# Norms pinned in program order, gate matmuls spread out, and list numbers multiplied in on ScalarE: one edit of a linear-attention and mixture-of-experts kernel

## The chip, the cores and the metric

The kernel runs on one core of a Trainium2 chip, with its engines TensorE (PE), VectorE (DVE), ScalarE (ACT), GpSimd (POOL) and SyncE (SP, which issues most DMAs). The metric is the device time of one execution in microseconds (us), the median of several runs. Every engine takes its instructions in the order of the built program, so an instruction that waits holds up those behind it on its engine.

## The reference

The input `x` is 8 x 512 x 512 (batch, token, channel), float32. All of it is computed in float32:

```python
xn = layernorm(x)
# attention, 16 heads of 32, in chunks of 128 tokens
q, k, v = rotate(silu(xn @ Wq)), rotate(silu(xn @ Wk)), xn @ Wv
o = lightning_attention(q, k, v)          # per chunk: (q k^T * decay) v + (q * decay) state
o = group_rmsnorm(o * sigmoid(xn @ Wg1 @ Wg2)) * norm_weight
s = o @ Wo
# mixture: 16 experts, 4 per token, and one shared expert
probs = softmax(xn @ gate_w.T); top 4, weights normalised to 1
mixed = sum over experts of weight * (silu(xn @ Wg) * (xn @ Wu)) @ Wd
g = silu(mixed + shared(xn) * sigmoid(xn @ shared_gate_w))
return x + s * g
```

There are 4096 tokens, so 16384 pairs of token and expert.

## The kernel before

The program is one stream of helper calls that a scheduling layer turns into one queue per engine. The order of PE's matmuls is written out by hand: `on_pe` ties each to the matmul traced before it. On the other engines the layer may reorder, by its own reckoning of when an instruction becomes ready, unless a helper says `behind(engine)`, which ties an instruction to the last one traced on that engine. Accumulators in PSUM come from `bank(tag, ...)`: tag `a` has four banks, `d` two, `m` and `k` one each. A matmul into a bank waits until whoever read its last content is done.

**Stage 1, to about 220 us.** For each batch `b`, `first()` yields pieces: `route_1` (router logits, L305, copied to `lT` at L309), `share_1` (the shared expert's gate and up matmuls, L358, with silu on ACT and the product `h` on DVE, L364), `norm(b + 2)`, `turn(b + 1)` (transposes, L289, copied by ACT at L291), `route_2` (top 4, softmax and one-hot masks: L317 to L348) and `share_2` (L374, four tiles of tokens whose results `sh` are taken out by ACT for even tiles, L380, and by DVE for odd ones, L378, then written to DRAM). `norm` computes statistics on DVE (L250, L252), the inverse root on POOL (L254, L256), and centres on DVE (L242). `along()` hands out nine pieces for every five calls, between the pieces of the first batch's attention: `value(0, t)` for four tiles (L574), then the gates `gate_1`, `gate_2`, `gate_3` of batch 0 (L587, L596, L608, results copied or put through a sigmoid by ACT: L591, L598, L611), then `enter` and `sequence(0)`: keys and queries (L619, silu at L624, rotation on DVE at L626 to L630), `by_token` (L646, L649), `scores` (L664, L675, and on DVE L678, L680, L685, L691), `output` (L703, L709, and on DVE L713). In `norm`, `stand` ties the instructions of batches 0 and 1 with `behind`, those of later batches not.

`sort()` then gives each pair its place in a list ordered by expert, in blocks of 128.

**Stage 2, about 249 to 330 us.** `table(room)` turns places into `slot`, the token that stands at each place. There are 128 lists (4 ranks x 32 tiles of 128 tokens), in 8 groups of 16. For each group `make` builds on DVE, in f16, one-hot rows of the place within a block (`place`, L510: 1024 wide for 8 lists), multiplies them by the token number (L512), and builds one-hot rows of the block (`block`, L515: 1144 wide); the lists lie next to each other, so one list's row is every fourth element. PE multiplies `place` by `block` per list (L534, into `pn`, bank `a`) and DVE adds the groups up (L540, L542). Two groups have room at a time. `filling` is the generator of all this, and `between[0]` advances it once after each matmul of `value` and `rotated`, inside `sequence(1)`. `sequence(1)` begins with `scores(1, 0)`, goes on with `key(1, 2)`, and then calls `gate_3(1)`, which needs four banks `a` that the scores have just used.

```python
        make(0)
        for _ in range(KC + 1):
            yield
        for i in range(0, TOPK * NT, GROUP):
            if i + GROUP < TOPK * NT:
                make(i + GROUP)
```

**Afterwards** the expert weights (`wexp`, loaded while stage 2 runs) are applied to 136 blocks of gathered rows (L1026 to L1097), and the attention of batches 2 to 7 runs on PE while gathered expert results are added up and joined with it (L1164 to L1202).

Of the kernel before, what the change touches and what calls it, by code (L numbers as in the profile page):

```python
# [11 lines left out]
F16 = mybir.dt.float16  # L12
# [4 lines left out]
ALU = mybir.AluOpType  # L17
# [34 lines left out]
def shape_constants():  # L52

    f = np.float32
    c = {}
    lam = -(f(2.0) ** (f(-8.0) * (np.arange(H, dtype=f) + f(1.0)) / f(H))).astype(f)
    i = np.arange(C, dtype=f)
    diff = i[None, :] - i[:, None]
    dec = np.exp(lam[None, :, None] * np.maximum(diff, f(0.0))[:, None, :])
    c["dmask"] = np.where(diff[:, None, :] >= 0, dec, f(0.0))  # L60
    dq = np.exp(lam[:, None] * (i[None, :] + f(1.0)))
    c["dq"] = np.repeat(dq.reshape(G, HG, 1, C), HD, axis=2).reshape(G, P, C).transpose(1, 0, 2)
    c["dk"] = np.exp(lam[None, :] * (f(C) - f(1.0) - i[:, None]))
    lc = np.exp(lam * f(C))
    c["lamc"] = np.repeat(lc.reshape(G, HG, 1), HD, axis=2).reshape(G, P).T
    half = HD // 2
    theta = (f(BASE) ** (f(-2.0) * np.arange(half, dtype=f) / f(HD))).astype(f)
    ang = (np.arange(N, dtype=f)[None, :] * theta[:, None]).astype(f)
    c["cos"] = np.tile(np.cos(ang), (2 * HG, 1))
    c["sin"] = np.tile(np.concatenate([-np.sin(ang), np.sin(ang)], axis=0), (HG, 1))  # L70
    c["ident"] = np.eye(P)


    sel = np.zeros((P, H - HG + Q))
    exp = np.zeros((H, G, P))
    for g in range(G):
        for j in range(HG):
            sel[j * HD : (j + 1) * HD, H - HG + j] = 1.0 / HD
            exp[g * HG + j, g, j * HD : (j + 1) * HD] = 1.0
    c["sel"] = sel  # L80

    c["four"] = np.tile(np.eye(Q), (P // Q, P // Q))
    c["fold"] = np.tile(np.eye(Q)[:, :EA], (P // Q, 1))

    c["tri"] = np.triu(np.ones((P, P)), 1)
    c["iota_e"] = np.tile(np.arange(E), (P, 1))
    c["reset"] = np.tile((np.arange(NT) > 0)[None], (P, E)).reshape(P, E * NT)
    out = {k: np.ascontiguousarray(v.reshape(P, -1), dtype=f) for k, v in c.items()}
    out["exp"] = exp.reshape(H, D).astype(f)
    out["iota_b"] = (np.arange(P, dtype=f)[:, None] // Q * NBQ + np.arange(NBQ, dtype=f)).astype(f)  # L90

    out["whole"] = np.tile(np.arange(NB), (P, 1)).astype(np.float16)
    out["token"] = (
        np.arange(NT)[None, :] * P + np.arange(P)[:, None] - B * N // 2).astype(np.float16)
    return out


# [1 line left out]
def tile_block(ctx: ExitStack, tc: tile.TileContext, a: dict, out: bass.AP):  # L99
# [8 lines left out]
    def bank(tag, name):  # L108
        return pp.tile([P, 512], F32, tag=tag, name=name, bufs={"a": 4, "k": 1, "m": 1, "d": 2}[tag])
# [9 lines left out]
    def load(pool, name, shape, dt=F32):  # L119
        t = pool.tile(shape, dt, tag=name, name=name, bufs=1)  # L120
        flat = t if len(shape) == 2 else t.rearrange(
            "p a b -> p (a b)" if len(shape) == 3 else "p a b c -> p (a b c)")
        nc.sync.dma_start(flat, a[name])
        return t
# [36 lines left out]
    iota_e = load(p1, "iota_e", [P, E])  # L161
    tri = load(p1, "tri", [P, P])
    reset = load(p1, "reset", [P, E * NT])
    token = load(const, "token", [P, NT], F16)
    whole = load(const, "whole", [P, NB], F16)
    iota_b = load(p1, "iota_b", [P, NBQ])
    ones = p1.tile([P, P], F32, tag="ones", name="ones")
# [48 lines left out]
    def behind(engine):  # L216

        last = next(
            (i for i in reversed(nc.cur_bb.bb.instructions) if i.engine == engine), None)
        return tc.issue_after(last) if last else nullcontext()  # L220
# [9 lines left out]
    def norm(b):  # L230
        xs = xs_of[b]
        mv = p1.tile([P, NC, 2], F32, tag="mv", name=f"mv_{b}", bufs=2)
        rstd = p1.tile([P, NC], F32, tag="rstd", name=f"rstd_{b}", bufs=2)
        tiles = [slice(t, t + 1) for t in range(NC)] if b == 0 else [slice(0, NC)]

        def stand(engine):
            return behind(engine) if b < 2 else nullcontext()

        def center(ts):
            for t in range(ts.start, ts.stop):  # L240
                with stand(DVE):
                    nc.vector.tensor_scalar(  # L242
                        xs[:, t, :], xs[:, t, :], mv[:, t, 0:1], rstd[:, t : t + 1],
                        ALU.subtract, ALU.mult)

        for i, ts in enumerate(tiles):
            for t in range(ts.start, ts.stop):
                st = p1.tile([P, 6], F32, tag="st", name=f"st_{b}_{t}", bufs=4)
                with stand(DVE):
                    nc.vector.bn_stats(st, xs[:, t, :])  # L250
                with stand(DVE):
                    nc.vector.bn_aggr(mv[:, t, :], st)  # L252
            with stand(POOL):
                nc.gpsimd.tensor_scalar(rstd[:, ts], mv[:, ts, 1], LN_EPS, None, ALU.add)  # L254
            with stand(POOL):
                nc.gpsimd.tensor_tensor(  # L256
                    rstd[:, ts], rstd[:, ts],
                    root.to_broadcast([P, ts.stop - ts.start]), ALU.pow)
            if i:
                center(tiles[i - 1])  # L260
        center(tiles[-1])
        nc.sync.dma_start(
            xn_d[b * N : (b + 1) * N, :D].rearrange("(t p) d -> p t d", p=P),
            xs[:, :, : D // 2].bitcast(U16))
# [102 lines left out]
    def share_2(b):  # L367
        h, sg = h1_of.pop(b), sg_of.pop(b)
        xT1_of.pop(b)
        for t in range(NC):  # L370
            sh = p1.tile([P, D], F32, tag="sh1", name=f"sh1_{b}_{t}", bufs=6)
            py = bank("dmaa"[t], f"pys_{b}_{t}")
            with on_pe():
                nc.tensor.matmul(  # L374
                    py, lhsT=h[:, t * P : (t + 1) * P], rhs=sw[:, KC * 2 * F :],
                    start=True, stop=True)
            if t % 2:
                nc.vector.tensor_scalar(sh, py, sg[:, t : t + 1], None, ALU.mult)  # L378
            else:
                nc.scalar.activation(sh, py, AF.Copy, scale=sg[:, t : t + 1])  # L380
            nc.sync.dma_start(sh_d[b][t * P : (t + 1) * P, :], sh)
# [91 lines left out]
    def table(room):  # L473
# [26 lines left out]
        def make(i):  # L500
            place, block = homes[i // GROUP % 2]
            for u in range(0, quads, 2):
                us = slice(u, u + 2)
                lists = slice(i + u * QUAD, i + (u + 2) * QUAD)
                first = lists.start % NT

                def counts(n):
                    return count[:, :n].unsqueeze(1).to_broadcast([P, 2, n, QUAD])

                nc.vector.tensor_tensor(  # L510
                    place[:, us], counts(P), rows(sp[:, 0, lists], P), ALU.is_equal)
                nc.vector.tensor_tensor(  # L512
                    place[:, us], place[:, us], rows(token[:, first : first + 2 * QUAD], P),
                    ALU.mult)
                nc.vector.tensor_tensor(  # L515
                    block[:, us], counts(NB), rows(sp[:, 1, lists], NB), ALU.is_equal)

        make(0)
        for _ in range(KC + 1):
            yield  # L520
        for i in range(0, TOPK * NT, GROUP):
            if i + GROUP < TOPK * NT:
                make(i + GROUP)
            else:
                for e in range(E - LATE, E - LATE // 2):
                    nc.sync.dma_start(wexp[:, e, :], a["experts"][:, e, :])
            if i < TOPK * NT // 2:
                yield
            place, block = homes[i // GROUP % 2]
            pn = bank("a", f"pn_{i}")  # L530
            for some in ((0, 5), (5, 10), (10, GROUP)):
                with on_pe():
                    for j in range(*some):
                        nc.tensor.matmul(  # L534
                            pn[:, :NB], lhsT=place[:, j // QUAD, :, j % QUAD],
                            rhs=block[:, j // QUAD, :, j % QUAD], start=(j == 0),
                            stop=(j == GROUP - 1))
                if some[1] == GROUP:
                    if i:
                        nc.vector.tensor_tensor(acc, acc, pn[:, :NB], ALU.add)  # L540
                    else:
                        nc.vector.tensor_copy(acc, pn[:, :NB])  # L542
                yield
# [427 lines left out]

    for t in range(NC):
        value(0, t)
        along()
    gate_1(0)
    gate_2(0)
    gate_3(0)
    along()
    enter(0, along)
    sequence(0, along, spill, also=lambda: next(sorting, None))  # L980
# [323 lines left out]
```

## Time and profile before

| what | value |
|---|---|
| runs | 1227.79, 1227.75, 1227.76 us, median 1227.76 |
| the profiled execution | 1224.5 us, of which the span from first to last instruction 1222.7 |
| granted TensorE clock, mean over the span | 0.991 |
| PE busy, 0 to 400 us | 373.3 us |
| DVE busy, 240 to 300 us | 53.6 of 60 us |
| ACT busy, 240 to 300 us | 10.7 of 60 us |

Busy time is the time in which an engine executes; a share of the span averages over stages with different limits. A row of instructions gives line, engine, operation, output and inputs, shape and number, then busy time and mean duration in ns, then the idle time of the engine just before them and what ended it. A row of waits gives who waited, for whom, the total in us, how often, and the longest. In the view of single stretches the columns are the stretch, its length, then busy time and number of instructions for PE, PE's weight loads, DVE, ACT and POOL, then the granted clock of TensorE (1.00 is full), the busy share of the DMA engines and GB/s. In the timeline a row begins with its start and its duration in us, and ends with the idle time before it in brackets.

### The profile page before, as it was taken

The numbers are of one execution on the slowest core, as the hardware profiler recorded it, in microseconds if no ns is written. First come the engines' busy times: TensorE is split into PE (matmuls) and PEld (weight loads), VectorE is DVE, ScalarE is ACT, GpSimd is POOL, SyncE is SP. The second block draws the span as 40 slices with busy tenths as digits, with TensorE's granted clock in tenths as the row PEclk, the third lists the DMA queues.
The fourth block names the chain that finished last, engine by engine and source line by source line (L and its number), as shares of the span: only waits on it lengthen the run. The fifth ranks groups of instructions, "written<-read, shape, count | busy, mean of one in ns | idle before, by whom it ended". The sixth has DMA issues, their size and how long they took to land. (4 is left out here: it accounts for less than half of the span.)

```text
span 1222.7 us, 21290 instructions
## 1 busy us (share of the span) xinstructions
PE 1171.0 (96%) x7708; PEld 688.6 (56%) x7708; DVE 758.6 (62%) x1632; ACT 407.2 (33%) x767; POOL 438.3 (36%) x424
## 2 busy tenths in 40 slices
PE   6998999989999999999999999999999999999997
PEld 3434554446567777777777775545544444445453
DVE  6487554889324344444444435959879689698784
ACT  3343333320274344444444432041141221411420
POOL 3122002100213333333333332832876837848211
PEclk9998999989999999999999999999999999999999
DMA  9884231182459989889998996822746626535012
GB/s 320 292 282 159 100 138 70 27 326 96 156 139 224 223 227 227 223 229 230 228 229 226 229 222 223 295 62 70 261 119 191 197 79 228 162 111 149 25 36 69
DMA packets 163352, 216.97 MB, mean 177 GB/s; under 512 B 89776, under 2 KB 98736, under 8 KB 161328
## 3 DMA queue, kind: packets, MB, share of 16 engines
q1 hardware_dynamic: 141840, 143.68, 38.9%
q0 software_dynamic: 21120, 70.34, 21.0%
q8 instruction: 64, 1.05, 0.4%
q10 hardware_dynamic: 288, 1.57, 0.4%
q14 instruction: 40, 0.33, 0.1%
HBM read 125.35 MB, written 72.35 MB: 162 GB/s over the span
## 5 line engine op out<-in xcount | busy, mean ns | idle before, releaser
L1067 PE MATMUL pgu<-wexp,xt 128*128 x1088 | 257.7, 380 | 2.3 <-ACT xt L1048 2.0
L1067 PEld LDWEIGHTS pgu<-wexp,xt 128*128 128x128 f32 x1088 | 206.0, 190 | 89.5 <-issue 43.2
L1026 POOL DMA_INDIRECT xg<-xn_d,slot x79 | 75.1, 951 | 249.8 <-DVE y L1097 163.5
L1072 DVE TENSOR_TENSOR slb<-slb,pgu 128x128 f32<-128x128 f32 x136 | 39.1, 288 | 191.0 <-ACT slb L1071 124.3
L1164 POOL DMA_INDIRECT yg<-y_d,posi x128 | 139.5, 1090 | 47.1 <-SPq L1131 19.5
L1050 ACT COPY xt<-pl 128x512 uint16<-128x512 uint16 x136 | 104.3, 767 | 126.9 <-DMA pl<-xg 70.3
L1088 PE MATMUL py<-wexp,hT 128*128 x272 | 139.3, 594 | 0.1
L574 PE MATMUL pv<-wv,xT 128*128 128x512 f32 x256 | 122.1, 613 | 4.4 <-DVE sh L378 3.0
L619 PE MATMUL pk<-xT,wk 128*128 128x512 f32 x256 | 118.3, 604 | 1.7 <-DVEq L1131 1.7
L619 PE MATMUL pq<-xT,wq 128*128 128x512 f32 x256 | 117.6, 600 | 0.0
L1196 POOL TENSOR_TENSOR xo<-xo,m 128x512 f32<-128x512 f32 x30 | 43.4, 1448 | 164.9 <-DVE m L1192 155.9
L752 PE MATMUL pw<-wo,on 128*128 128x512 f32 x224 | 100.5, 595 | 0.8 <-DVE m L1192 0.6
L1026 POOL DMA_INDIRECT more<-xn_d,slot x57 | 54.0, 947 | 109.7 <-DVE y L1097 106.8
L574 PEld LDWEIGHTS pv<-wv,xT 128*128 128x128 f32 x256 | 46.7, 195 | 59.9 <-issue 53.2
L691 DVE TENSOR_TENSOR sc<-ps,dmask 128x512 f32<-128x512 f32 x128 | 79.4, 680 | 1.0 <-PE ps L675 1.0
L619 PEld LDWEIGHTS pq<-xT,wq 128*128 128x128 f32 x256 | 47.8, 193 | 52.8 <-issue 51.7
L1097 DVE TENSOR_SCALAR y<-py,xg 128x512 f32<-128x512 f32 x79 | 59.3, 750 | 28.4 <-PE py L1088 28.0
L619 PEld LDWEIGHTS pk<-xT,wk 128*128 128x128 f32 x256 | 46.1, 190 | 52.0 <-issue 49.6
L752 PEld LDWEIGHTS pw<-wo,on 128*128 128x128 f32 x224 | 41.4, 190 | 50.5 <-issue 45.2
L1071 ACT ACTIVATE slb<-pgu 128x128 f32<-128x128 f32 x136 | 37.8, 278 | 90.9 <-PE pgu L1067 87.8
L578 ACT COPY v<-pv 128x512 f32<-128x512 f32 x32 | 18.9, 590 | 122.6 <-PE pv L574 121.8
L624 ACT ACTIVATE sk<-pk 128x512 f32<-128x512 f32 x32 | 19.1, 596 | 117.0 <-PE pk L619 100.1
(168 smaller groups left out, 1787.5 us busy)
## 6 DMA issues: line engine op xcount, KB each, us to landing
y_d<-y SPq DMA_DIRECT2D x136, 256.0 KB
wexp<-in_experts SPq DMA_DIRECT2D x14, 768.0 KB
sh_d<-sh SPq DMA_DIRECT2D x32, 256.0 KB
m<-sh_d SPq DMA_DIRECT2D x32, 256.0 KB
xo<-in_x SPq DMA_DIRECT2D x32, 256.0 KB
out<-xo SPq DMA_DIRECT2D x32, 256.0 KB
x<-in_x SPq DMA_DIRECT2D x7, 1024.0 KB
xT_d<-xT SPq DMA_DIRECT2D x7, 1024.0 KB
```

Source lines behind the costliest of these rows:

```text
L574: nc.tensor.matmul(pv, lhsT=xT_of[b][:, k, t * P : (t + 1) * P], rhs=wv[:, k, :], start=(k == 0), stop=(k == KC - 1))
L619: nc.tensor.matmul(ps, lhsT=w[:, k, g * P : (g + 1) * P], rhs=xT_of[b][:, k, :], start=(k == 0), stop=(k == KC - 1))
L691: nc.vector.tensor_tensor(s, pss[j].rearrange("p (c t) -> p c t", t=C), dmask[:, g * HG + j].unsqueeze(1).to_broadcast([P, NC, C]), ALU.mult)
L752: nc.tensor.matmul(pw, lhsT=on_of[b][:, g, t * P : (t + 1) * P], rhs=wo[:, g, :], start=(g == 0), stop=(g == G - 1))
L1026: nc.gpsimd.indirect_dma_start(out=row(i), out_offset=None, in_=xn_d, in_offset=bass.IndirectOffsetOnAxis(ap=slot[:, i : i + 1], axis=0))
L1050: nc.scalar.copy(xt[:, KP:, :].bitcast(U16).rearrange("p k (t h) -> p h k t", h=2), turned(i).rearrange("p (h k) t -> p h k t", h=2))
L1067: nc.tensor.matmul(pg[:, : 2 * F], lhsT=xt[:, k, :], rhs=wflat[:, bass.ds(off + k * 2 * F, 2 * F)], start=(k == 0), stop=(k == KC - 1))
L1072: nc.vector.tensor_tensor(sl, sl, pg[:, F : 2 * F], ALU.mult)
L1088: nc.tensor.matmul(py, lhsT=hT_of.pop(i), rhs=wflat[:, bass.ds(off_of.pop(i) + KC * 2 * F, D)], start=True, stop=True)
L1097: gone.append(nc.vector.tensor_scalar(y, py, row(i).bitcast(F32)[:, bass.ds(at, 1)], None, ALU.mult).ins)
L1164: nc.gpsimd.indirect_dma_start(out=yg, out_offset=None, in_=y_d, in_offset=bass.IndirectOffsetOnAxis(ap=posi[:, r, g : g + 1], axis=0))
L1196: nc.gpsimd.tensor_tensor(xo, xo, m, ALU.add)
```

## The change

Five edits. `norm` ties its instructions for every batch, with `behind` in place of `stand`. `share_2` takes its banks in the order `dama` in place of `dmaa`, so the tile in bank `m` is an even one. `gate_1(0)`, `gate_2(0)` and `gate_3(0)` are called after `value(0, 1)`, `value(0, 2)` and `value(0, 3)`, each ahead of `along()`, in place of all three after the last. The multiplication by the token number leaves `make`; `number` does it on ACT, one activation of 128 x 128 per list, with the token's number (now float32) as the scale: for the first group four lists at a time, one call per step, and for later ones along with the matmuls of the group before. And `filling` yields once ahead of `make(0)`, so its first step builds no rows; the steps that follow are one fewer.

```diff
     out["token"] = (
-        ... .astype(np.float16)
+        ... .astype(np.float32)
@@ norm
-        def stand(engine):
-            return behind(engine) if b < 2 else nullcontext()
-
         def center(ts):
             for t in range(ts.start, ts.stop):
-                with stand(DVE):
+                with behind(DVE):
...
-            with stand(POOL):
+            with behind(POOL):
@@ share_2
-            py = bank("dmaa"[t], f"pys_{b}_{t}")
+            py = bank("dama"[t], f"pys_{b}_{t}")
@@ table: make
-                nc.vector.tensor_tensor(
-                    place[:, us], place[:, us], rows(token[:, first : first + 2 * QUAD], P),
-                    ALU.mult)
@@ table
+        def number(i, some):
+            place = homes[i // GROUP % 2][0]
+            for j in range(*some):
+                row = place[:, j // QUAD, :, j % QUAD]
+                t = (i + j) % NT
+                nc.scalar.activation(row, row, AF.Copy, scale=token[:, t : t + 1])
+
+        yield
         make(0)
-        for _ in range(KC + 1):
+        for j in range(0, GROUP, QUAD):
+            number(0, (j, j + QUAD))
             yield
         for i in range(0, TOPK * NT, GROUP):
-            if i + GROUP < TOPK * NT:
+            more = i + GROUP < TOPK * NT
+            if more:
                 make(i + GROUP)
...
+                if more:
+                    number(i + GROUP, some)
                 if some[1] == GROUP:
@@ the calls of stage 1
     for t in range(NC):
         value(0, t)
+        if t:
+            (gate_1, gate_2, gate_3)[t - 1](0)
         along()
-    gate_1(0)
-    gate_2(0)
-    gate_3(0)
     along()
```

More of the change, by code (lines that the diff above doesn't have):

```diff
@@ L93, in shape_constants @@
     out["token"] = (
-        np.arange(NT)[None, :] * P + np.arange(P)[:, None] - B * N // 2).astype(np.float16)
+        np.arange(NT)[None, :] * P + np.arange(P)[:, None] - B * N // 2).astype(np.float32)
     return out
@@ L163, in tile_block @@
     reset = load(p1, "reset", [P, E * NT])
-    token = load(const, "token", [P, NT], F16)
+    token = load(const, "token", [P, NT])
     whole = load(const, "whole", [P, NB], F16)
@@ L248, in norm @@
                 st = p1.tile([P, 6], F32, tag="st", name=f"st_{b}_{t}", bufs=4)
-                with stand(DVE):
+                with behind(DVE):
                     nc.vector.bn_stats(st, xs[:, t, :])
-                with stand(DVE):
+                with behind(DVE):
                     nc.vector.bn_aggr(mv[:, t, :], st)
-            with stand(POOL):
+            with behind(POOL):
                 nc.gpsimd.tensor_scalar(rstd[:, ts], mv[:, ts, 1], LN_EPS, None, ALU.add)
-            with stand(POOL):
+            with behind(POOL):
                 nc.gpsimd.tensor_tensor(
@@ L504, in make @@
                 lists = slice(i + u * QUAD, i + (u + 2) * QUAD)
-                first = lists.start % NT
                 def counts(n):
```

## The prediction

> **What bounds the kernel.** I read the busy shares first, then what TensorE (PE) waited for in the two stretches that the diff touches, then the granted clock around the longest waits, and last the queues of VectorE (DVE) and ScalarE (ACT) there.
>
> ```profile
> PE 1171.0 (96%) x7708; PEld 688.6 (56%) x7708; DVE 758.6 (62%) x1632; ACT 407.2 (33%) x767; POOL 438.3 (36%) x424
> ```
>
> PE is busy for 1171.0 of 1222.7 us, so a change can only win back PE's idle time and the time at a lower clock. The chain of waits of this profile holds the last instruction alone and tells nothing, so I go by PE's waits (total, times, longest), first from 20 to 112 us and from 100 to 140, then from 249 to 330:
>
> ```profile
> PE pv L574 <- DVE sh L378: 2.3, 1, 2.3
> PE psT L289 <- ACT on L611: 0.8, 1, 0.8
> PE pf L596 <- ACT g L591: 0.7, 1, 0.7
> PE p L608 <- ACT g L598: 0.7, 1, 0.7
> PE pys L374 <- ACT sk L624: 0.4, 1, 0.4
> ...
> PE ps L675 <- DVE sh L378: 3.3, 1, 3.3
> ```
> ```profile
> PE p L608 <- DVE sc L691: 2.6, 1, 2.6
> PE ps L675 <- DVE sc L691: 1.5, 1, 1.5
> PE pv L574 <- DMA xT<-xT_d: 1.4, 1, 1.4
> PE pn L534 <- DVE sc L691: 1.0, 1, 1.0
> ```
>
> The clock view of single stretches (PE, PEld, DVE, ACT, POOL busy, then PEclk) shows a second price of such waits:
>
> ```profile
> 26.07:29.48 3.41, 1.75 (x5) 0.44 (x3) 3.22 (x24) 2.83 (x5) 0.00 (x0) 1.00 1.09 395
> 107.99:111.40 3.41, 1.16 (x40) 0.93 (x32) 3.41 (x8) 0.00 (x0) 0.00 (x0) 1.00 0.25 97
> 111.40:114.81 3.41, 2.37 (x20) 2.37 (x20) 2.80 (x10) 0.00 (x0) 0.00 (x0) 0.50 0.41 154
> 254.76:258.17 3.41, 1.10 (x3) 0.58 (x4) 3.41 (x8) 1.88 (x2) 0.00 (x0) 1.00 1.03 410
> 258.17:261.58 3.41, 3.41 (x11) 1.72 (x9) 3.41 (x8) 2.38 (x4) 0.00 (x0) 0.50 1.02 425
> ```
>
> A stretch of 3.41 us in which PE is busy for a third is followed by half clock, for 6.83 us both times (111.40 to 118.23, 258.17 to 265.00); one with 1.75 us busy is not.
>
> **The change part by part**, in times of this profile. Where I name what an instruction waits for in the new program, it is from the built program's order and semaphores.
>
> *A, banks of `share_2` (`dama`).* The 2.3 us wait of `pv` is for bank `m`, which DVE empties (L378) behind the second norm. In the new order ACT empties it, and the table load and `e` that stood ahead of its two `sh` (26.85 to 28.27) now stand behind them. DVE's norm no longer holds back `lg`, so `sg` comes at 25.6 (the end of its table load), and the second `sh` when PE has its tile, 26.9 to 27.6. PE is done with `pys` at 27.8 and goes on: **-2.3**.
>
> *B, gates between pieces.* The waits 0.70 + 0.68 + 0.77 = 2.15 us go: `gate_1` and `gate_2` now have 3.5 us and more of other matmuls behind them. But `gate_3` comes straight behind `pv` of tile 3, and in ACT's queue its sigmoids stand behind that tile's copy (0.59) and a table load (1.28). The fourth `p2` waits for the first sigmoid's bank, `plT` for the second's, and `pg` of the shared expert for bank `m`, whose `sh` is now queued behind all four sigmoids. From the end of `pv`: 0.6 + 1.28 + 4 x 0.52 + 0.65 = 4.6 us until `pg` may start, of which PE works 0.9 + 0.4 (`p2`) + 1.0 (`plT`): 2.3 us idle. **+0.15** in all, a wait for a wait. Half clock behind it would add 1.7; the stretch is about half busy, so I leave it out.
>
> *C.* `pys` no longer waits for `sk` (tile 2 reaches bank `m` 0.9 us later): **-0.4**. PE is now 2.5 us ahead.
>
> *D, norms hold their place.* Here is the 3.3 us wait:
>
> ```profile
> 107.36 1.29 DVE L250 BATCH_NORM_STATS2 st<-x 128x6 f32<-128x512 f32 x2 [3.01 <-DMA x<-in_x]
> ```
>
> Statistics of batch 7 wait for their DMA at the head of DVE, and behind them `swq`, `qT` and two `sh` that PE needs. In the new order this norm comes some 40 us later and waits for nothing. But the norm of batch 5 now stands right there, between `lg` and `swq`. DVE's walk: rotation of `k` ends 98.45 (2.5 us early); four statistics with eight small searches between them, 3.5; `kd` and two small ones, 0.65; POOL's gap before L242 is 1.49 from the last aggregate, so centring starts at 103.45 and takes 1.9 to 3.1 (rows of both); one-hots 0.6, small ones 0.4, `swq` 107.4 instead of 108.58; six more of 0.6 to 0.66 with small ones, `lT` done at 111.4. PE reaches `ps` at 105.7 and idles nearly 5 us, but `pg` starts at 111.7, not 115.04: 3.3 us ahead, 0.8 more than before the stage. Half clock costs before 1.6 us after 115.04; now 3.41 us of it from 111.4, 1.7, so no difference: **-0.8**. The later norms fall into stages where DVE has slack; in batch 6's, statistics 2.8, POOL's gap 1.5 and centring 2.2 now stand ahead of `kd`, a rotation and L713, which ends 1.3 us after PE could start `pys` (0.8 now), and the `sh` behind it some 0.2: **+0.7**.
>
> *E, one-hot rows.* DVE loses 16 multiplications:
>
> ```profile
> L512 DVE TENSOR_TENSOR wexp<-wexp,token 128x1024 f16<-128x1024 f16 x16 | 11.0, 684 | 0.0
> L691 DVE TENSOR_TENSOR sc<-ps,dmask 128x512 f32<-128x512 f32 x16 | 10.1, 680 | 0.0
> ```
>
> ACT gains 128 multiplications of 128x128 f16, each a row of every fourth element. No row shows that; the neighbours are:
>
> ```profile
> L1050 ACT COPY xt<-pl 128x512 uint16<-128x512 uint16 x136 | 104.3, 767 | 126.9 <-DMA pl<-xg 70.3 <-DMA pl<-more 54.6 <-issue 1.6
> L1071 ACT ACTIVATE slb<-pgu 128x128 f32<-128x128 f32 x136 | 37.8, 278 | 90.9 <-PE pgu L1067 87.8 <-issue 2.8
> L380 ACT ACTIVATE sh<-pys,sg 128x512 f32<-128x512 f32 x16 | 10.5, 680 | 4.3 <-PE pys L374 2.5 <-issue 1.7
> L727 ACT ACTIVATE rs<-pr,eps_rms 128x128 f32<-128x128 f32 x7 | 2.6, 367 | 0.1
> ```
>
> Two `sh` of 0.68 took 1.25 together, so neighbours overlap by 0.11. Bounds of the step from one list to the next: 0.278 - 0.11 = 0.17 (same width, no per-partition operand) and 0.767 (strided 16-bit, four times as wide). I take the row nearest in shape and operand, 0.367 - 0.11, plus 0.03 for reading SBUF (L720's 0.632 against L624's 0.597): **0.29**. 128 x 0.29 = 37 us, in a stretch of 75 us where ACT works 3.7 of 35; the total is covered, the order is not.
>
> The name of the edit promises the first scores ahead of the first rows. The new order of DVE doesn't give that: four pairs of comparisons, both first groups, still stand ahead of `sc`. They take 4 x (0.60 + 0.66) + 0.4 = 5.4 us from 249.70 against 6.6 now, so `gate_3` starts at 255.9 instead of 257.07. Then ACT: 32 list multiplications stand ahead of `sk`, a table load and `on`, and the first `pn` needs the bank that the first `on` empties. The first comparison ends at 250.3; 250.3 + 32 x 0.29 + 0.5 (`so`) + 0.6 + 1.28 + 0.6 = 262.6. PE is there at 260.1 (full clock) and waits 2.5 us; before, `pn` starts at 264.97. So 2.3 us are won, and the stretch before 262 is again idle enough for half clock, at least 3.41 us at 1.7. **-0.6**. Later groups have their rows 2 us and more before PE asks. DVE's one-hots ahead of the last scores shrink, and of the 1.5 us wait of `ps` 0.3 is left: **-1.2**. The waits for `xT` and of the second `pn` stay.
>
> The Trainium skill, "ScalarE: Activation LUTs", section "Rules for kernel authors", speaks against this part: multiplication belongs on VectorE. The trace agrees on the price (0.60 us for eight lists on DVE, 2.3 on ACT); by that rule E is a plain loss, by the queues it is not, since ACT idles.
>
> The Trainium skill, "TensorE: Matmul & The Clock Gate", section "Why this matters for your kernels", allows PE gaps up to about 3 us before the clock halves. In this trace a gap of 2.55 us was enough. By the rule the new 2.5 us wait costs no clock, E's first part is -2.3 and the time 1221.7; I go by the trace.
>
> **Sum:** -2.3 + 0.15 - 0.4 - 0.8 + 0.7 - 0.6 - 1.2 = -4.4 us. The profiled execution took 1224.5 us (span 1222.7 and 1.8 around it), which would become 1220.1. The median of the runs, 1227.76, lies 3.3 above it; with the same difference, **1223.4**. After 330 us the orders agree and PE stays the bound, so the gain is kept.
>
> **Rivals.** (1) *No new wait at `pn`*: a step of 0.17 to 0.2. Then `pn` starts at 260.1, 4.9 early and without half clock, 4.3 better than forecast: 1219.1; without half clock at the norm too, 1217.5. For it: the 0.278 row. Against: the per-partition operand costs 0.09 in every pair of rows. (2) *A wait for a wait*: one or two of the three new idle spots get half clock of 6.83 us instead of 3.41 or none (1.7 each), as both had in this trace: 1225.5 to 1227.5, no change that could be told. (3) *Slower: ACT before the first `pn`.* If strided 16-bit rows cost 0.6 each, 32 of them put `pn` at 250.3 + 19.2 + 3.0 = 272.5, 7.5 late, plus 1.7 of clock, less the 3.8 of the other parts: +5.4, 1233. It turns the gain to nothing at 0.43 and shows as slower from 0.51; at 0.767 all 128 (98 us) outlast the stretch of 75 and cost some 20.
>
> **Numbers.** Forecast 0.42, (1) 0.22, (2) 0.22, (3) 0.14. A measurement here tells about 0.2%, 2.5 us. Faster: forecast nearly whole and (1), 0.62; within, (2) and edges, 0.24; slower 0.14. The range runs from the best of (1) past (2) and leaves out (3): 1217.5 to 1229.5.
>
> **What would show it.** Right: no idle before `pv` at 28; `pg` waiting some 2 us for an ACT `sh` near 60; PE idle about 5 us before `ps` near 106, released by DVE `lT` or `sh`; ACT `wexp` of 128x128 near 0.37 us; the first `pn` waiting for ACT `on`. Wrong: `wexp` steps beyond 0.43, half clock at other places, or waits of `pn` for ACT in the later groups.

## The result, and the profile after

The change made no difference that can be measured. In 14 runs each, taken side by side, the changed kernel has a median of 1224.2 us (1220.18 to 1229.64) and the kernel before 1225.76 us (1216.62 to 1229.44); the means differ by 0.1 us, and the ratio of the times is 1.0001, with a 95% interval of [0.9982, 1.0019]. Single runs lie up to 12.8 us apart before and 9.5 us after, so the three runs first shown, 0.04 us apart, told nothing of that spread. The forecast was 1223.4 us as a time, and the median lies 0.8 us from it; but it was also a gain of 4.4 us (0.36%), and no such gain is there.

The profiled execution of the changed kernel took 1228.5 us, its span 1226.7, at a mean granted clock of 0.984 (before 1224.5, 1222.7 and 0.991). PE's busy time grew by 3.1 us, although it does the same number of matmuls; ACT took over 44.7 us of work:

```profile
PE 1174.1 (96%) x7708; PEld 691.4 (56%) x7708; DVE 750.9 (61%) x1616; ACT 451.9 (37%) x898; POOL 439.8 (36%) x424
```

PE's waits in the changed kernel, from 20 to 112 us and then from 100 to 140:

```profile
PE ps L680 <- DVE sh L375: 3.4, 1, 3.4
PE p L613 <- ACT on L616: 1.5, 1, 1.5
PE pg L355 <- ACT sh L377: 0.2, 1, 0.2
```
```profile
PE pys L371 <- DVE on L718: 2.9, 1, 2.9
```

The wait of `pv` (2.3) and the three of 0.7 to 0.8 at the gates are gone. In their place stand 1.5 for `gate_3`'s bank and 2.9 for `pys`, and the wait of `ps` is as long as it was (3.4, before 3.3). From 249 to 330 us:

```profile
PE p L613 <- DVE sc L696: 1.4, 1, 1.4
PE pv L579 <- DMA xT<-xT_d: 1.3, 1, 1.3
PE pn L537 <- DVE sc L696: 1.1, 1, 1.1
PE ps L680 <- DVE sc L696: 0.8, 1, 0.8
PE pn L537 <- ACT on L616: 0.6, 1, 0.6
...
```

Here the gain came: 1.4 instead of 2.6 for `p`, 0.8 instead of 1.5 for `ps`, against 0.6 new for the first `pn`. What the other waits cost beyond themselves stands in the view of single stretches (PE, weight loads, DVE, ACT, POOL, then the granted clock):

```profile
57.57:60.98 3.41, 1.90 (x10) 0.45 (x10) 1.98 (x4) 3.17 (x6) 1.94 (x3) 1.00 0.54 156
60.98:64.39 3.41, 3.23 (x8) 1.38 (x5) 1.35 (x2) 1.72 (x2) 0.00 (x0) 0.50 0.84 186
105.35:108.76 3.41, 1.18 (x20) 0.96 (x8) 3.41 (x15) 1.41 (x2) 1.08 (x2) 1.00 0.81 281
108.76:112.17 3.41, 2.21 (x13) 2.21 (x15) 3.41 (x7) 0.00 (x0) 0.00 (x0) 0.50 0.72 263
115.59:119.00 3.41, 3.41 (x5) 1.35 (x4) 0.00 (x0) 0.00 (x0) 0.00 (x0) 0.50 0.00 0
136.07:139.48 3.41, 1.39 (x3) 0.68 (x4) 3.31 (x14) 1.88 (x3) 0.00 (x0) 1.00 0.01 2
139.48:142.90 3.42, 3.42 (x6) 1.34 (x4) 2.22 (x4) 1.14 (x2) 0.00 (x0) 0.50 0.20 77
258.95:262.36 3.41, 3.28 (x12) 1.60 (x13) 1.87 (x4) 3.41 (x14) 0.00 (x0) 1.00 0.94 357
262.36:265.77 3.41, 3.41 (x6) 1.07 (x5) 1.22 (x4) 3.39 (x8) 0.00 (x0) 0.50 1.01 411
```

Each of the three new or kept waits before 140 us is followed by half clock: 3.41 us from 60.98, 10.24 from 108.76, 3.41 from 139.48. Before, there were 6.83 us in this part of the program, from 111.40.

Where PE stands at the same work shows where the gain was lost (start in us from the span's start):

| PE begins | before | after | ahead | ahead by the forecast |
|---|---|---|---|---|
| first `pv` of tile 2 behind `pys` | 30.11 | 26.31 | 3.8 | 2.3 |
| `psT` of batch 3 | 71.72 | 69.87 | 1.9 | 2.15 |
| first `pq` | 82.17 | 79.38 | 2.8 | 2.5 |
| `pg` of batch 4 | 115.04 | 113.83 | 1.2 | 3.3 |
| `pk` of group 2 | 125.32 | 125.10 | 0.2 | 3.3 |
| scores (1, 0) | 249.39 | 252.55 | -3.2 | 2.65 |
| first `pn` | 264.97 | 266.47 | -1.5 | 3.25 |
| behind stage 2 | 341.92 | 342.84 | -0.9 | 4.45 |
| end of the span | 1222.7 | 1226.7 | -4.0 | 4.4 |

Each column is one execution, and 1.4 us of every lead were there before the change could act: the first `pu` begins at 18.15 us before and at 16.71 after, because the eight `pg` ahead of it take 4.87 and 3.70 us. In e5, which is the changed kernel run again, they take 5.38 and `pu` begins at 18.97. Less these 1.4 us, PE is 2.4 us ahead at the first `pv` of tile 2, as the forecast had it, but 0.5 and 1.4 at `psT` and the first `pq` instead of 2.15 and 2.5.

Between the first `pq` and 250 us PE loses 6 us, in stage 2 it wins 2.3, and behind it the profile loses 3.1 more, in `pgu` waiting for ACT `xt` (4.3 us instead of 2.0) and in half clock at 682 and 754 us that the other profile did not have. That last loss is not shown to come from the change: in e5 the same `pgu` waits 2.4 us.

### The profile page after: what moved, and what is told of

Read it like the earlier page. It is cut to its first block, busy times and chain, and to the rows that moved or that the text cites. A ratio compares the mean times of both kernels' runs of the same rounds, so it can differ in the third digit from the quotient of the medians.

```text
span 1226.7 us, 21456 instructions
## 1 busy us (share of the span) xinstructions
PE 1174.1 (96%) x7708; PEld 691.4 (56%) x7708; DVE 750.9 (61%) x1616; ACT 451.9 (37%) x898; POOL 439.8 (36%) x424
## 3 DMA queue, kind: packets, MB, share of 16 engines
q0 software_dynamic: 21120, 70.34, 20.9%
## 5 line engine op out<-in xcount | busy, mean ns | idle before, releaser
L629 ACT ACTIVATE sk<-pk 128x512 f32<-128x512 f32 x32 | 19.2, 602 | 105.5 <-PE pk L624 92.0
L1101 DVE TENSOR_SCALAR y<-py,more 128x512 f32<-128x512 f32 x57 | 42.8, 750 | 22.2 <-PE py L1092 21.6
```

The lines of the kernel that those rows point to most:

```text
L1101: gone.append(nc.vector.tensor_scalar(y, py, row(i).bitcast(F32)[:, bass.ds(at, 1)], None, ALU.mult).ins)
```

## The experiments

Each run stood beside runs of the kernel before on the same chip; the four of a group share them. A line of the table stands for 12 runs, for e9 to e11 six, for the kernel before 35, 35 and 17. "Lost" is span times (1 - mean clock), the mean over the runs: half of the time at half clock. It is what half clock took only where PE would have been busy. "Full speed" is span times clock. Both are to be compared with the kernel before of the same group, since that alone went from 1210.2 to 1208.9 and 1209.6 in full speed.

| run | median us | ratio to before, 95% | full speed | lost |
|---|---|---|---|---|
| before, group 1 | 1227.77 | | 1210.2 | 16.0 |
| e1 banks | 1224.64 | 0.9968 [0.9948, 0.9988] | 1208.8 | 14.5 |
| e2 norms | 1232.1 | 1.0044 [1.0024, 1.0063] | 1211.5 | 19.2 |
| e3 gates | 1230.13 | 1.0021 [0.9993, 1.0049] | 1210.4 | 17.9 |
| e4 rows | 1223.06 | 0.9967 [0.9945, 0.9989] | 1210.3 | 11.9 |
| before, group 2 | 1224.85 | | 1208.9 | 14.4 |
| e5 the whole change | 1227.74 | 1.0012 [0.9986, 1.0039] | 1209.9 | 16.8 |
| e6 without the pins | 1224.08 | 0.9991 [0.9966, 1.0016] | 1209.4 | 13.5 |
| e7 pin of batch 2 alone | 1224.5 | 0.999 [0.9964, 1.0015] | 1208.0 | 14.6 |
| e8 the same, gates back | 1221.94 | 0.9968 [0.9941, 0.9995] | 1208.4 | 11.4 |
| before, group 3 | 1227.45 | | 1209.6 | 15.6 |
| e9 pins of 2 and 7 | 1217.83 | 0.9927 [0.9906, 0.9948] | 1206.2 | 9.9 |
| e10 second group behind | 1216.79 | 0.9914 [0.9896, 0.9933] | 1205.4 | 9.5 |
| e11 gates apart | 1218.21 | 0.9929 [0.9909, 0.995] | 1205.9 | 10.1 |
| e12 fill | 1226.37 | 0.9995 [0.9975, 1.0014] | 1210.2 | 14.5 |

The theory at the start: the waits are shifted rather than removed, and the half clock behind them eats the rest. Its rivals: one part costs what the others win, or the gain is there and hidden in the spread.

**e1, the banks alone.**

```diff
-            py = bank("dmaa"[t], f"pys_{b}_{t}")
+            py = bank("dama"[t], f"pys_{b}_{t}")
```

> The kernel before with the bank order of the shared expert's output alone changed (`dama`). I use one more number here, the full-speed time: span times mean granted clock, which takes the half-clock windows out (before, profiled: 1222.7 x 0.991 = 1211.7; after, 14 runs: 1205.0 to 1209.5). Theory (the waits go as forecast, the clock windows hide it): the 2.3 us wait of `pv` near 28 is gone, full-speed time 1209 to 1210, median 1223 to 1226 because single runs spread by 6 us. Rival (the gain arrives in the time): clock as before, median 1223.4 or less. Rival (the wait moves): `pv` or `lg` waits 2 us elsewhere before 60, full-speed time 1211 to 1212.

The wait near 28 us did not go; it changed its releaser (PE's waits from 10 to 40 us of this run):

```profile
PE pv L574 <- ACT sh L380: 2.9, 1, 2.9
```

So the third case holds for the wait, and the prediction's first step gave it to the wrong edit. The median is 3.1 us lower all the same. This profile doesn't explain it: its execution took 1228.94 us, near the top of the 12 runs. What these banks alone win, and by what, stays open.

The profile shows something else that matters below. The norms float here as before, yet `ps` waits only 0.7 us (3.3 before; 1.0 in e4, where they float too), and no half clock follows near 111 us in either. PE comes 2 us later (first `ps` at 110.19 instead of 108.22), and DVE waits less for batch 7's load:

```profile
107.17 1.29 DVE L250 BATCH_NORM_STATS2 st<-x 128x6 f32<-128x512 f32 x2 [0.84 <-DMA x<-in_x]
```

So the wait of 3.3 us with 6.83 us of half clock behind it is not a fixed cost of the kernel before; what is lost ahead of it can shrink it.

**e2, the norms alone.**

```diff
         def stand(engine):
-            return behind(engine) if b < 2 else nullcontext()
+            return behind(engine)
```

> The kernel before with the norms of batches 2 to 7 alone held in place in the queues. Theory (batch 5's norm takes the place of batch 7's DMA wait): PE still idles 3 to 5 us before `ps` near 108 with half clock behind it, `pys` near 130 waits 1.5 to 3 us instead of 0.8, full-speed time 1211 to 1213.5, median 1225.5 to 1228. Rival (the DMA wait at the head of VectorE was the cost): the wait before `ps` is under 1 us, no half clock near 111, full-speed time 1208 to 1209, median 1221 to 1222.5.

This is the part that costs: 4.3 us by the median, beyond the theory's own range; 3.2 of it are lost to the clock (19.2 against 16.0). The wait of `pv` near 28 is gone here, with the old banks: batch 2's pin removes it, not the bank order. PE's waits from 100 to 145 us of this run:

```profile
PE ps L672 <- DVE sh L375: 4.4, 1, 4.4
PE pys L371 <- DVE on L710: 2.9, 1, 2.9
```

Both are longer than in the profile before (3.3 and 0.8). What stands ahead of `ps` shows in DVE's timeline of the changed kernel, where the four pieces of batch 5's centring end the norm:

```profile
97.80 0.69 DVE L247 BATCH_NORM_STATS2 st<-x 128x6 f32<-128x512 f32 x1
...
101.48 0.54 DVE L654 TENSOR_TENSOR kd<-pk,dk 128x384 f32<-128x384 f32 x1
102.90 2.51 DVE L239 TENSOR_SCALAR x<-x,mv,rstd 128x512 f32<-128x512 f32 x4 [0.87 <-POOL rstd L253]
...
107.01 0.71 DVE L631 STREAM_SHUFFLE swq<-sq 128x512 f32<-128x512 f32 x1
```

`swq` starts at 107.01; what PE needs stands 4 to 5 us behind it. The same happens to batch 6's norm ahead of `pys`, with 1.48 us for POOL in it:

```profile
124.23 0.69 DVE L247 BATCH_NORM_STATS2 st<-x 128x6 f32<-128x512 f32 x1
...
129.00 2.50 DVE L239 TENSOR_SCALAR x<-x,mv,rstd 128x512 f32<-128x512 f32 x4 [1.48 <-POOL rstd L253]
```

**e3, the gates alone.**

```diff
         value(0, t)
+        if t:
+            (gate_1, gate_2, gate_3)[t - 1](0)
         along()
-    gate_1(0)
-    gate_2(0)
-    gate_3(0)
```

> The kernel before with the first batch's three gate steps alone spread between the value matmuls (bank order `dmaa` as before). Theory (a wait for a wait): the three waits of 0.7 each near 52 to 58 go, `p` of `gate_3` and `pg` or `plT` behind it wait 1.5 to 2.5 us together near 60, full-speed time 1211 to 1212, with a half-clock window near 61 to 64; median 1225 to 1227.5. Rival (the gate steps are hidden for nothing): no wait over 0.5 us between 40 and 66, full-speed time 1209.5, median 1223.5.

The wait of `p` came as the theory had it (40 to 100 us), and half clock with it, 6.83 us from 63.45; a longer wait for `sk`, 1.1 us instead of 0.4, came on top:

```profile
PE p L608 <- ACT on L611: 1.5, 1, 1.5
PE pys L374 <- ACT sk L624: 1.1, 1, 1.1
```
```profile
60.04:63.45 3.41, 1.88 (x7) 0.74 (x8) 2.20 (x8) 3.38 (x5) 1.03 (x2) 1.00 0.80 185
63.45:66.86 3.41, 3.41 (x12) 0.53 (x10) 3.14 (x5) 2.59 (x4) 3.05 (x5) 0.50 1.03 426
66.86:70.27 3.41, 3.41 (x5) 1.34 (x5) 1.49 (x3) 0.00 (x0) 0.00 (x0) 0.50 1.04 392
```

The median is 2.4 us up, above the theory's range of 1225 to 1227.5, though the interval of the ratio reaches below 1. PE is busy for 55% of the stretch ahead; "about half busy" was no reason to leave the clock out. The profile before had already shown such a case, with half clock from 790.65:

```profile
787.24:790.65 3.41, 1.71 (x37) 1.37 (x41) 1.36 (x3) 0.00 (x0) 2.78 (x4) 1.00 0.90 324
```

**e4, the rows alone.** The diff is that of `table` in the change.

> The kernel before with the one-hot part alone: ScalarE multiplies the rows list by list, and one more yield ahead of the first rows. Theory (list steps of 0.31 us are covered, the first `pn` comes earlier or at the same time): first `pn` 1 to 2.5 us ahead of its place in the kernel before, `ps` waits 0.7 less, full-speed time 1208.5 to 1210, median 1222.5 to 1224.5. Rival (ScalarE's 128 multiplications are the cost that ate the gains of the other parts): first `pn` later than 264.97 or new waits of `pn`, `pg` or `p2` for ACT after 265, full-speed time 1212 or more, median 1227 or more.

4.7 us down, with the median inside the theory's range of 1222.5 to 1224.5, and in the mean all of it is clock (lost 11.9, before 16.0; full speed 1210.3, before 1210.2, where the theory had 1208.5 to 1210). PE's waits for `sc` (145 to 345 us) fall to the same 1.4 and 0.8 as in the changed kernel; none for ACT's multiplications is over 0.5 us:

```profile
PE p L616 <- DVE sc L699: 1.4, 1, 1.4
...
PE pn L540 <- DVE sc L699: 1.2, 1, 1.2
PE ps L683 <- DVE sc L699: 0.8, 1, 0.8
```

The rival, ScalarE as the cost, falls. The four medians add up to -1.1 us: the norms and the gates take back what banks and rows give. Each is uncertain by 2.4 to 3.4 us to either side, so the sum fits no change at all, but does not prove it.

**e5, the whole change again.** The kernel of the change, without an edit.

> The changed kernel once more, beside the kernel before on the same chip. The medians of the parts alone came out -3.1 us (banks), +4.3 (norms), +2.4 (gates) and -4.7 (rows), together -1.1. Theory (gains and losses of the parts cancel): ratio 0.997 to 1.001, full-speed time (span times mean clock) 1206.5 to 1207.5 against 1210.2 of the kernel before, but some 18 us of half clock as before. Rival (the forecast gain is there, and the first comparison missed it by its spread): ratio 0.994 to 0.9965.

1.0012, just beyond the theory's range on the slow side: the rival, a gain of 0.35% hidden in the spread, falls. A part of the theory falls too. The full-speed time is 1209.9, not 1206.5 to 1207.5, and no lower than the 1208.9 of the kernel before beside it: that the waits had shrunk in sum and half clock alone hid it is not so. I had compared numbers of different groups of runs.

**e6 and e7, pins taken back.** The changed kernel with `b < 2` (e6) and with `b < 3` (e7):

```diff
+        def stand(engine):
+            return behind(engine) if b < 3 else nullcontext()
```

> The changed kernel without the norms' pin (batches 2 to 7 float again): banks, gates and rows together. Theory (the pin is the part that costs): the 2.9 us wait of `pys` near 132 shrinks to 0.8, the wait of `ps` near 106 varies with the load of batch 7 as in the kernel before (0.7 to 3.3), the wait of `pv` near 28 is back (2 to 3 us), median 2 to 4 us below the changed kernel: 1221 to 1223. Rival (the pin is what makes the bank order pay): `pv`'s wait comes back and nothing goes, median 1225 to 1227.

> The changed kernel with only batch 2's norm pinned, batches 3 to 7 floating as before. Theory (batch 2's pin takes away `pv`'s wait at 28, the pins of batches 5 and 6 cost at `ps` and `pys`): no wait of `pv` near 28, `pys` near 132 waits under 1.2 us, full-speed time 1204.5 to 1206.5, median 1220.5 to 1222.5. Rival (PE, 2 to 3 us ahead, now runs into batch 7's load at the head of VectorE): `ps` waits 3 to 6 us near 106, median 1224 to 1226.

The waits did what the theory said: `pv` waits 2.2 us near 28 in e6 and not in e7, and `pys` waits 0.8 in both. The times did not follow: 0.9991 and 0.999, a miss. `ps` still waits 2.1 us in e6 and 2.2 in e7, with 6.83 us of half clock behind it, and e7's median lies in its rival's range. DVE still waits there for batch 7's load (1.86 us in e7), as that rival said, though `ps` waits less than its 3 to 6 us.

**e8, gates back.** As e7, with the three gates behind the four `value` again.

> As the run before, and the first batch's gate steps are put back behind the four value matmuls. Theory (spreading the gates costs half clock near 61): no half clock near 61, the three waits of 0.7 near 50 to 58 are back, median 1 to 2.5 us below the run before: 1218.5 to 1221. Rival (the gates are a wait for a wait and nothing more, +0.15): within 1 us of the run before.

No half clock near 61 us, and 2.6 us less than e7; lost goes from 14.6 to 11.4. It fits e3, though the intervals overlap. What still holds PE near 107 is plain in its DVE timeline: statistics of batch 7, at the head of the queue, wait for their load. That load was issued at 97.36 here and at 101.11 in e4, but the statistics start at 105.31 and 107.17: of 3.75 us by which PE is ahead, half is left.

```profile
105.31 1.29 DVE L250 BATCH_NORM_STATS2 st<-x 128x6 f32<-128x512 f32 x2 [2.66 <-DMA x<-in_x]
```

**e9, the pins of batches 2 and 7.**

```diff
-            return behind(engine) if b < 3 else nullcontext()
+            return behind(engine) if b < 3 or b == B - 1 else nullcontext()
```

> As the kernel with batch 2's norm pinned and the gates put back, and batch 7's norm pinned too; batches 3 to 6 float. Theory (of the pins, those of batches 2 and 7 pay and those of 5 and 6 cost): VectorE's 2.7 us wait for the load of batch 7 is gone, PE's wait of `ps` near 108 is under 1.2 us and no half clock follows there, `pys` near 130 waits 0.8; full-speed time 1205 to 1207, median 2 to 5 us below the 1221.94 of the kernel without the pin of 7 if the two chips' kernels before agree. Rival (another queue is late there): `ps` still waits 2 us, for ScalarE or for another norm, and the median stays within 1.5 us.

The theory in full, and the largest gain so far: 0.9927. `ps` waits 0.3 us (100 to 145 us), and no half clock follows:

```profile
PE pys L374 <- DVE on L721: 0.8, 1, 0.8
PE ps L683 <- DVE lT L309: 0.3, 1, 0.3
```
```profile
104.00:107.41 3.41, 3.41 (x15) 1.14 (x17) 2.45 (x5) 2.43 (x4) 0.00 (x0) 1.00 1.01 414
107.41:110.82 3.41, 3.14 (x61) 2.75 (x54) 2.96 (x8) 0.00 (x0) 0.00 (x0) 1.00 0.65 246
110.82:114.24 3.42, 3.42 (x9) 1.51 (x9) 2.10 (x4) 0.00 (x0) 0.00 (x0) 1.00 0.00 1
```

Of the mean's 9.1 us against the kernel before, 3.4 are full speed and 5.6 clock.

**e10, the second group of rows behind the scores.** `make`'s two comparisons with `behind(DVE)` for every group but the first:

```diff
+                with behind(DVE) if i else nullcontext():
                     nc.vector.tensor_tensor(place[:, us], ...)
```

> As the run before, and the comparisons of every group of one-hot rows but the first hold their place in VectorE's queue. In the built order 2 pairs instead of 4 then stand ahead of the first scores' `sc`, and 17 instead of 33 list multiplications ahead of ScalarE's `sk` and `on`. Theory (order, not the cost of a multiplication, is what holds PE there): the wait of `p` for `sc` (1.4) is under 0.4, the first `pn` waits less than 1 us for `on`, full-speed time 1.5 to 3 us below the run before. Rival (the second group is then late): the second `pn` group waits 1 to 3 us more for rows, no gain.

`p` no longer waits, and `pn` no longer for `on` (2.3 in e9), but the wait is met again later, for DVE (145 to 345 us):

```profile
PE pn L542 <- DVE sc L701: 3.5, 1, 3.5
```

1.4 + 2.3 + 1.1 became 3.5. The median is 1.0 us lower, within the intervals: mostly a wait for a wait. At 0.9914 it is the lowest of all kernels here, but not told apart from e9.

**e11, two gates apart.** As e10, with `gate_1` and `gate_2` behind the second and third `value`, `gate_3` behind all.

> As the run before, and the first batch's gate_1 and gate_2 go between the value matmuls while gate_3 keeps its old place behind them. Theory (the gain of spreading is the 1.4 us of `pf` and `p`; what costs is gate_3's sigmoids ahead of the shared expert's copies): waits of 0.7 for `g` gone, no wait of `p` for `on` over 0.3, no half clock near 61; median 0.5 to 2 us below the run before. Rival: a new wait of 1 us and more between 40 and 66 takes its place, median equal or above.

The rival, though later than it said: the waits of `pf`, `p` and `psT` (0.7, 0.7, 0.8) go, `p` waits 0.4 for another, and `pys`, near 78 us, waits 1.9 for `sk` instead of 0.7. No half clock near 61, no gain.

**e12, work laid into the gap.**

```diff
+            for _ in range(10 if b == 0 and g == 0 else 1):
                 for c in range(NC - 1):
```

> The changed kernel with the 12 small matmuls of the first scores' state (`pk`) done ten times over instead of once: the same values, 108 matmuls more, about 0.3 us per 12 by the trace, so some 3 us of work laid into the 3.4 us in which PE idles ahead of `ps` near 106. Theory (an idle of that length costs half clock behind it, 10.2 us of it in the profile of the changed kernel): no half clock between 106 and 125, or 3.4 us at most, and a median 3 to 5 us below the changed kernel in spite of the added work. Rival (the half clock comes from something else, or small matmuls do not hold the clock): 7 to 10 us of half clock at the same place, median equal or up to 1 us above.

It didn't decide what it should. The ten repeats took 2.35 us, not 3, all before the wait, which stayed at 2.15 us and a second one of 0.78:

```profile
103.06:106.47 3.41, 3.41 (x250) 2.73 (x250) 3.41 (x12) 2.50 (x4) 2.17 (x4) 1.00 0.59 199
106.47:109.89 3.42, 0.64 (x4) 0.29 (x2) 3.42 (x9) 0.00 (x0) 0.00 (x0) 1.00 0.84 298
109.89:113.30 3.41, 3.27 (x29) 2.77 (x30) 2.25 (x7) 0.00 (x0) 0.00 (x0) 0.50 0.35 129
113.30:116.71 3.41, 3.41 (x5) 1.35 (x4) 1.51 (x3) 0.00 (x0) 0.00 (x0) 0.50 0.00 0
```

Half clock is 6.83 us instead of 10.24, the median not told apart from the changed kernel. What it shows is that 3.4 us of full work straight ahead doesn't save the clock when the stretch behind it is mostly idle.

Its first 100 us are those of the changed kernel, with the same wait of 1.5 us of `p`. Here the wait (57.78 to 59.30) lies across the border of two stretches, and no half clock follows:

```profile
55.28:58.69 3.41, 2.50 (x10) 0.67 (x8) 2.79 (x6) 1.91 (x3) 2.77 (x4) 1.00 0.01 3
58.69:62.10 3.41, 2.53 (x11) 0.75 (x12) 1.69 (x5) 3.16 (x6) 1.04 (x2) 1.00 0.76 175
62.10:65.51 3.41, 3.41 (x9) 1.52 (x8) 0.74 (x2) 0.92 (x2) 0.00 (x0) 1.00 0.92 264
```

The Trainium skill, "TensorE: Matmul & The Clock Gate", section "Why this matters for your kernels", allows PE gaps up to about 3 us. In this run gaps of 2.15 and 0.78 us, which share one stretch, were enough for 6.83 us of half clock, and the same gap of 1.5 us was followed by 3.41 us of it in the changed kernel and by none here. The length of a gap alone does not tell what follows in these runs.

## Where the prediction held and where it failed, step by step

It named the right queues and nearly every new wait, and the median came within 1 us of the forecast time. That was luck: the base of 1227.76 was 2.0 us above the median of 14 runs, and the gain of 4.4 us is not there. The step that failed is **D**, the norms, with **B** behind it; in both, the half clock behind a wait was sized from one profile or left out.

- **A** (-2.3): the wait is gone, and PE was 3.8 us ahead there, of which 1.4 stood before the change could act. The reason was half wrong: with these banks alone it stays (e1, 2.9 for ACT), with the norms alone it goes (e2). It belongs to batch 2's pin, so to D.
- **B** (+0.15, clock left out): the waits were 1.5 + 0.2 where 2.3 was forecast, but the half clock that was set aside came, 3.41 us in the profile of the change and 6.83 in e3, e5, e6 and e7. PE's lead fell from 3.8 to 1.9 us, +1.9 instead of +0.15. Alone it cost 2.4 us by the median (e3, interval across 1).
- **C** (-0.4): right; `pys` doesn't wait for `sk` in the changed kernel.
- **D** (-0.8, then +0.7): the walk along DVE was right to 0.4 us (`swq` at 107.4 forecast, 107.01 measured). What was mis-sized is what follows. PE idled 3.44 us where nearly 5 was forecast, but 10.24 us of half clock came behind it instead of 3.41: up to 5.1 us lost against the 1.7 counted. `pys` behind batch 6's norm waited 2.9 us instead of 1.5, with half clock from 139.48 that was not counted; in e2 and e5 the same wait of 2.9 has none behind it. And the wait that was to be won was taken as fixed, where e1 and e4 show it at 0.7 and 1.0 with the norms still floating. PE was 3.2 us behind at the scores of batch 1, where the forecast had it 2.65 ahead. Alone the norms cost 4.3 us by the median, with an interval clear of 1 (e2).
- **E** (-0.6 and -1.2): right in sum; from the scores to the end of stage 2 PE gains 2.3 us. It is split the other way round: from the first `ps` of scores (1, 0) to the first `pn` PE takes 13.60 us instead of 15.26, a gain of 1.7, and 0.6 came behind it. ACT's list takes 0.31 us per step (23 in 7.16 us), forecast 0.29; the rows that bounded it told the step but not the duration, 0.56 us, since neighbours overlap by 0.25 and not 0.11:

```profile
256.92 7.16 ACT L516 ACTIVATE wexp<-wexp,token 128x128 f16<-128x128 f16 x23
```

  The Trainium skill, "ScalarE: Activation LUTs", section "Rules for kernel authors", would keep such a multiplication on VectorE; here its move to a mostly idle ScalarE, with one more yield, gave 0.9967 (e4), so the rule's price was not on PE's path. The prediction's 2.3 us for eight lists on ACT was its own estimate, not a reading of the trace; by the measured step it is 2.5. The first `pn` waited 0.6 us for `on`, not 2.5, because 3.41 us of half clock (from 262.36) stood ahead of it. In e8 and e9 no half clock stands ahead of it, it waits 2.3 us, and the 13.6 us from `ps` to `pn` are the same in all three. So half clock ahead of a wait for another engine cost nothing there, and the 1.7 counted for it was one charge too many.
- **The base** (+3.3 from the profiled execution to the median of the three runs): these lie 0.04 us apart, and the 14 runs of the same kernel 12.8. The median of the 14 is 1225.76, so the difference was 1.3.

Rival (2), "a wait for a wait, more half clock", at 0.22, is the case that came by its mechanism, though the median of 1224.2 lies below its 1225.5 to 1227.5. The forecast priced half clock once per place, from one profile. But much of the spread of the runs is the clock: of the 14 runs of the change, the shortest has a span of 1218.4 at 0.991, the longest 1227.8 at 0.983, so 11.0 and 20.9 us lost, and that 9.9 covers the whole difference of 9.4. It is not all of the spread: in e4 full speed alone goes from 1205.2 to 1215.8. The borders lie on a grid of 3.41 us (111.40 and 258.17 in the profile before are 43 stretches apart), which has another place in every profile here. The same wait of 1.5 us of `p` has 3.41 us of half clock behind it in the changed kernel, 6.83 in e3, e5, e6 and e7, and none in e12.

What the change could have given is in e9: the pins of batches 2 and 7 with banks and rows, 0.9927. The waits ahead of `pv` and `ps` are gone in it, and none is added at `pys`. It differs from the change in the gates too, not only in the pins of batches 3 to 6. Which of these pins costs how much was not run apart; that those of 5 and 6 do is argued from e2, where all six together cost, and from the places of the waits. Whether e9 needs the banks or the rows was not tried either.

## What to carry to other kernels

Pin an instruction group in its queue only where the trace shows that it, floating, holds up what PE needs: all six new pins cost 0.44%, while one of them added to e8 went with a ratio of 0.9927 instead of 0.9968 (the two intervals just overlap), and the queue's head at the time of each wait told which to try. A gain ahead of a later wait for a load is swallowed there in part, so try a part again once the later wait is gone. Price every PE wait with the half clock that may follow it, over several runs, and take the spread from more than three runs before turning microseconds into chances.

## What the runs showed of the hardware

In most of the views shown here half clock came after a stretch of 3.41 us in which PE was busy for 0.19 to 0.56 of the time, also where no single wait was over 1.5 us (57.57 to 60.98 in the changed kernel: 1.90 busy). That is no bound. One with 1.89 us busy in the same profile (344.28 to 347.70) had full clock behind it, and the half clock from 262.36 came after a stretch with 3.28 us busy, with 2.14 in the one ahead of that. Half clock lasted 3.41, 6.83 or 10.24 us, in the changed kernel the longest where the first stretch at half clock had idle time too (2.21 of 3.41 busy); in the profile before, 2.37 busy there went with 6.83. A set of 12 matmuls of 128x32 by 32, done ten times over, took 2.35 us, so 0.235 us a set, where the single set took 0.37.

128 multiplications of 128x128 f16 with a scale per partition, every fourth element, took 42.3 us of ACT's time. PE never waited for them directly; the first `pn` waits 0.6 us in the changed kernel and 2.3 in e9 for `on`, which stands behind 32 of them in ACT's queue:

```profile
L516 ACT ACTIVATE wexp<-wexp,token 128x128 f16<-128x128 f16 x128 | 42.3, 563 | 12.6 <-DVE wexp L506 12.6
```
